# All fronts first, and two turns beside other stages, in a hybrid scan, convolution and attention kernel

## The chip, the cores and the metric

The kernel runs on one core of one Trainium2 chip. The metric is the device time of one execution in microseconds; the median of several runs is given.

## The reference

Four images of 96 channels and 64 x 64 pixels go through four layers. Only the first layer matters in detail here.

```python
# layer 0: x + conv_ref(group_norm(x))
u = silu(depthwise3x3(einsum('oc,bchw->bohw', Win, x)) + conv_b)      # 192 channels
xs = stack([u, u.T, flip(u), flip(u.T)])                              # 4 directions k
dts, Bs, Cs = split(einsum('bkdl,ked->bkel', xs, sel_w))              # 6 + 16 + 16
delta = softplus(dt_w @ dts + dt_b)
h[t] = h[t-1] * exp(delta * A) + (delta * u) * B[t]                   # 4096 steps, 192 x 16 states
y[k] = sum_n h * C
y = y0 + y1.T + flip(y2) + flip(y3).T + D * xs                        # directions summed
x = x + Wout @ layer_norm(y)
# layer 1: 1x1 convolution, depthwise 3x3, 1x1 convolution, residual
# layer 2: Fourier transform along the tokens, diagonal product, inverse, residual; quantised feed-forward
# layer 3: linear attention (k^T v first), residual; quantised feed-forward
```

## The kernel before

**The scan** is the backbone. For each image, direction and chunk of 512 positions there is a step (32 steps an image), and each step has 12 units of work. A unit makes two state tiles: POOL multiplies rep_g with rep_BC (L1266), ACT takes an exponential into PSUM (L1276), DVE runs the recurrence (L1285), DVE (L1290) or POOL (L1306) multiplies with C, and PE sums the states into ps_y (L1330). This makes 1536 units. Image 0's scan takes units 0 to 383, image 1's the next 384, and so on; directions go 0, 1, 3, 2, and 1, 3, 0, 2 for the last image. delta, du (delta times u), B and C are written to DRAM by the fronts and fetched from there, repeated over partitions, as rep_d, rep_g and rep_BC.

**The order is written out by hand.** `scans()` goes through the units; one pass of its loop is a slot. In each slot it emits the scan's own instructions, and then hands what is left to a planner. The planner holds a list of stages, and each stage a list of streams, generators that yield how much time of an engine the next piece takes (`pe(2.7, 1)`: 2.7 us of TensorE, one PSUM bank; `wait(10)`: not before ten slots later). Only the first stage of the list is worked on; up to `width` streams of it are active, the earlier ones first. A piece is emitted when the engine's allowance permits it. All engines and the SP queue keep the emitted order.

```python
RATE = 6.0                                                        # us of planned work a slot
SHARE = {"pe": (3.0, 3.2), "act": (2.4, 2.8), "dve": (1.5, 2.0)}  # gain a slot, most held
BANKS = {"mm": 3, "da": 4, "y": 1}                                # PSUM banks
```

**The stages of an image:** front (input convolution with the group norm, L550 and L559; then scan inputs, L588 to L627: sel and dt products, softplus on ACT and DVE, and stores of delta, du, bc), turn (the transposed directions 1 and 3 are put into row order, and directions 0 and the skip added), conv (scan outputs L697, output norm, layer 1's expansions L787 and rows L810), spectral twice and layer_2 (layer 2), product, layer_3.

**What holds a stage back.** `scanned[b]` counts the finished steps of image b. A turn waits until 24 steps are done (16 for the last image, whose second row group then waits piece by piece for up to 24). Chunk c of conv's scan outputs waits for 32 - c steps. Front(3) could not be placed before the end of image 0's scan, since delta, du and bc had three DRAM sets and image 3 used image 0's.

**A turn** has three row groups r of 64 channels. For each it loads the y rows of directions 1 and 3 into a buffer `ya` (two loads of 1 MB, L640), waits ten slots, and for each of eight chunks fetches rows of direction 0 and of the skip (L649, L650), makes two products into one bank (L655: the transposed read of `ya`; L657: the skips), copies the result on ACT (L661) and stores it.

**After the scan** the rest of image 3 (what is left of its conv, then layers 2 and 3) runs with all PSUM banks; this is called the tail.

Before the change the stage list is: rest of front(0), weights and group norm statistics, front(1), front(2), turn(0), conv(0), layers 2 and 3 of image 0, front(3), turn(1), conv(1), layer 2 of image 1, layer_3(1) with turn(2), conv(2), layer 2 of image 2, layer_3(2) with turn(3), conv(3); then the tail.

Of the kernel before, what the change touches and what calls it, by code (L numbers as in the profile page):

```python
# [27 lines left out]
B, C, H, W = 4, 96, 64, 64  # L28
L = H * W
K, NS, R, DI = 4, 16, 6, 192  # L30
# [3 lines left out]
CH = 512  # L34
NCH = L // CH
RPC = CH // W
# [15 lines left out]


WORK = {"weights": 47.0, "turn": 79.2, "front": 417.0, "conv": 447.0,
        "spectral": 111.2, "layer_2": 231.0, "product": 1.2, "layer_3": 153.6, "layer_3_turn": 232.8}
RATE = 6.0
SHARE = {"pe": (3.0, 3.2), "act": (2.4, 2.8), "dve": (1.5, 2.0)}
NQ, NG, NPAIR = 4, HID // 32, H // 2
# [37 lines left out]
def hybrid_kernel(ctx: ExitStack, tc: tile.TileContext, a: dict):  # L96
# [5 lines left out]
    mm = nc.tensor.matmul  # L102
    act = nc.scalar.activation
    load = nc.sync.dma_start
# [37 lines left out]
    def const(name, rows=slice(0, 128)):  # L142
        return cst[rows, CS[name]]
# [40 lines left out]
    def big(name):  # L184
        if last_room and turns(thirds) == "last":
            return last_room[0].tile([128, 6144], F32, name=name, tag="big", bufs=1)
        return bp.tile([128, 6144], F32, name=name, tag="big", bufs=2)
# [20 lines left out]
    def images(name, shape, zero=None, sets=2):  # L208

        out = []  # L210
        for i in range(sets):
            t = dram1.tile(shape, F32, name=f"{name}{i}")
            if zero is not None:
                zero(t)
            out.append(t)
        return out

    d_delta = [images(f"delta{k}_", [NCH, DI, CH], sets=3) for k in range(K)]
    d_du = [images(f"du{k}_", [NCH, DI, CH], sets=3) for k in range(K)]
    d_bc = [images(f"bc{k}_", [NCH, 2 * NS, CH], sets=3) for k in range(K)]  # L220

# [10 lines left out]
    def split(t):  # L234
        return t.rearrange("p (a b) -> p a b", a=RPC)
# [341 lines left out]

    def scan_inputs(b, u, o, c, done):

        i = b % 3  # L580
        if not done.issuperset([c] if o == 0 else range(NCH)):
            while not done.issuperset([c] if o == 0 else range(NCH)):
                yield wait(1)
            yield wait(2)
        ua, ub = u
        yield pe(1.8, 1)
        p = bank()
        mm(p, lhsT=sel[:, o, 0, :], rhs=view(ua, o, c), start=True, stop=False)  # L588
        mm(p, lhsT=sel[:, o, 1, :], rhs=view(ub, o, c), start=False, stop=True)

        yield ac(0.7)
        xd = tmp("xd")
        act(xd, p, AF.Identity, bias=col("one"))
        free()
        for e in (0, 1):
            later(d_bc[o + 2 * e][i][c], xd[64 * e : 64 * e + 2 * NS])
        for part in range(3):
            yield pe(0.9, 1, part > 0)
            p = bank()
            if part < 2:  # L600
                mm(p, lhsT=dtw[:, o + 2 * part, 0:128], rhs=xd, start=True, stop=True)  # L601
                at = [(slice(0, 128), o + 2 * part, slice(0, 128))]
            else:
                for e in (0, 1):
                    mm(p[64 * e : 64 * e + 64], lhsT=dtw[:, o + 2 * e, 128:DI], rhs=xd, start=True, stop=True)
                at = [(slice(64 * e, 64 * e + 64), o + 2 * e, slice(128, DI)) for e in (0, 1)]

            yield ac(0.65)
            z = tmp("z")
            act(z, p, AF.Abs)  # L610
            yield ac(0.65)
            act(z, z, AF.Exp, scale=-1.0)
            yield ac(0.65)
            act(z, z, AF.Ln, bias=1.0)  # L614
            yield dv(0.7)
            nc.vector.scalar_tensor_tensor(p, p, 0.0, z, ALU.max, ALU.add)  # L616
            yield dv(0.85)
            g = tmp("g")
            nc.vector.tensor_mul(split(g), split(p), view(ub if part == 2 else ua, o, c))
            for rows, k, ch in at:  # L620
                later(d_du[k][i][c][ch], g[rows])
            yield ac(0.6)
            nc.scalar.copy(z, p)  # L623
            free(behind=True)
            for rows, k, ch in at:
                later(d_delta[k][i][c][ch], z[rows])
        traced[b].add((o, c))  # L627

    def turn(b):


        im = b % 2
        early = b == B - 1
        while scanned[b] < (2 if early else 3) * NCH:
            yield wait(1)
        t = big("ya")
        for r in (2, 0, 1) if early else (0, 1, 2):
            lo = 64 * r
            for at, k in ((0, 1), (64, 3)):
                load(t[at : at + 64, :L].rearrange("p (c l) -> p c l", c=NCH),  # L640
                     d_y[k][im][:, lo : lo + 64, :].rearrange("c p l -> p c l"))

            rows = not (early and r == 2)
            held = slice(0 if rows else 64, 128)

            def fetch(c):
                u = t[:, L + c % 4 * CH : L + c % 4 * CH + CH]
                if rows:
                    load(u[:64], d_y[0][im][c, lo : lo + 64])  # L649
                load(u[64:], d_skip[b][c, lo : lo + 64])  # L650
                return u

            def added(p, of):
                c, u = of
                mm(split(p[:64]), lhsT=const("two")[:, :64],  # L655
                   rhs=t[:, :L].rearrange("p (w h) -> p h w", h=H)[:, c * RPC : (c + 1) * RPC, :], start=True, stop=False)
                mm(p[:64], lhsT=skips[held, r], rhs=u[held], start=False, stop=True)  # L657

            def stored(p, of):
                s = tmp("yrow")[:64]  # L660
                nc.scalar.copy(s, p[:64])  # L661
                later(d_yt[im][of[0]][lo : lo + 64], s)

            chunks = ahead(1, fetch, range(NCH))

            ready = (lambda n: scanned[b] >= 2 * NCH + min(n + 2, NCH)) if early and rows else (lambda n: True)
            yield wait(10)
            yield from in_turn(chunks, pe(2.7, 1), added, ac(0.6), stored, ready=ready)
            yield wait(2)
# [399 lines left out]
    def layers_2_and_3(b):  # L1069
# [83 lines left out]
        else:  # L1153
# [1 line left out]
        return spectra + [  # L1155
            Stage("layer_2", 4 if b == B - 1 else 3, *(layer_2(c) for c in range(NCH))),
            Stage("product", 1, product()),
            Stage("layer_3", 4 if b == B - 1 else 3, *(layer_3(c) for c in range(NCH))) if b not in (1, 2) else
            Stage("layer_3_turn", 4, turn(b + 1), *(layer_3(c) for c in range(NCH))),
        ]  # L1160

    def front(b):


        u, there, done = [], set(), set()

        def memory():
            u.extend([big("ua")[:, :L], big("ub")[:, :L]])
            if b > 0:
                yield from normalised(b, arriving(b), there)  # L1170
                return

            chunks = [(c, fetch_image(b, c, tmp)) for c in range(NCH)]
            load(cst[:, CS["grp"]], a["cst"][:, CS["grp"]])
            load(cols, a["cols"])
            first_weights()
            yield from group_norm(b, chunks)
            yield from normalised(b, chunks, there)

        streams = [memory()]  # L1180
        for c in range(0, NCH, 2):
            streams.append(input_conv(b, u, c, there, done))
            for e in (c, c + 1):
                streams.append(scan_inputs(b, u, 0, e, done))
        streams += [scan_inputs(b, u, 1, c, done) for c in range(NCH)]
        return [Stage("front", 3 if b == 0 else 4, *streams)]


# [5 lines left out]

    def middle(b):

        return ([] if b >= 2 else [Stage("turn", 1, turn(b))]) + conv_block(b)

    def plan():

        stats = (group_norm(b, arriving(b)) for b in range(1, B))
        out = [Stage("weights", 2, later_weights(), *stats)] + front(1) + front(2)
        out += middle(0) + layers_2_and_3(0) + front(3)
        for b in (1, 2):
            out += middle(b) + layers_2_and_3(b)
        return out

    def scans(stages):
# [13 lines left out]
        for number, step in enumerate(steps):  # L1222
            step["at"] = number % (K * NCH)
            u = 0
# [6 lines left out]

        def load_states(step, j):
            t = pair("rep_BC")
            of = d_bc[step["k"]][step["b"] % 3][step["c"], 8 * j : 8 * j + 8].rearrange("(s e) l -> s (e l)", e=2)
            load(t.rearrange("p e l -> p (e l)"), of.unsqueeze(0).to_broadcast([32, 4, 2 * CH]))
            step["BC"][j] = t

        def load_channels(step, i, name):
            t = pair(f"rep_{name}")
            of = (d_delta if name == "d" else d_du)[step["k"]][step["b"] % 3][step["c"], 64 * i : 64 * i + 64]  # L1240
            load(t.rearrange("p e l -> p (e l)"),
                 of.rearrange("(p e) l -> p (e l)", e=2).unsqueeze(1).to_broadcast([32, 4, 2 * CH]))
            step[name][i] = t
# [399 lines left out]
```

## Time and profile before

| | |
|---|---|
| median of 3 runs | 6344.4 us (6340.63 to 6344.61) |
| the profiled execution | 6358.61 us, span 6356.8 us |
| granted TensorE clock, mean | 0.834 |
| last recurrence of the scan ends | 5911 us into the span |
| HBM read, written | 861.88 MB, 237.44 MB |
| DMA queue of SP | 54.3% of 16 engines |
| L1266, one per unit | 1536 at 2365 ns |
| L1276, two per unit | 3072 at 690 ns |
| L1285, two per unit | 3072 at 1204 to 1272 ns |

The span runs from the first to the last instruction of the program. Busy times are of one profiled execution; its own time is compared with its own span, and it lies 14 us above the median. A window of the profile gives busy times between two moments of the span, counted in us from its start.

### The profile page before, as it was taken

How to read it: one execution, taken by the hardware profiler on the slowest of the kernel's cores; microseconds unless marked ns; L12 is line 12 of the kernel's file. 1: busy time of each engine (PE TensorE's matmuls, PEld its weight loads, DVE VectorE, ACT ScalarE, POOL GpSimd, SP SyncE). 2: the span in 40 equal slices, each digit the busy share in tenths (PEclk: the TensorE clock that was granted, in tenths of full speed). 3: DMA queues.
4: the chain of work that ended last, by engine and by line, in shares of the span. 5: the costliest groups of instructions: out<-in, count | busy, mean ns of one | idle time of the engine just before them, and what ended most of it. 6: DMA issues, size and time to landing. Idle time of an engine off the chain costs nothing. (4 is left out here: it accounts for less than half of the span.)

```text
span 6356.8 us, 84759 instructions
## 1 busy us (share of the span) xinstructions
PE 4685.7 (74%) x27692; PEld 1723.3 (27%) x27692; DVE 5490.6 (86%) x6059; ACT 4191.3 (66%) x8072; POOL 5169.6 (81%) x2743
## 2 busy tenths in 40 slices
PE   6732767756888776686469878767898777679998
PEld 2100212201222642121012236321222552112274
DVE  4979898998999989989989998888999999889245
ACT  5743777765666677877546656767666667666435
POOL 4857878779999899987899998898999988889100
PEclk9855978867998888797779987878899887789999
DMA  5654565667754554456776445456754554566201
GB/s 178 206 167 146 190 204 187 201 201 221 221 162 151 183 181 156 151 193 208 212 213 197 156 152 192 157 162 199 225 171 159 171 192 141 172 209 202 84 13 39
DMA packets 430397, 1100.47 MB, mean 173 GB/s; under 512 B 74138, under 2 KB 75904, under 8 KB 428804
## 3 DMA queue, kind: packets, MB, share of 16 engines
q1 hardware_dynamic: 429956, 1095.06, 54.3%
q8 instruction: 220, 3.60, 0.2%
q14 instruction: 221, 1.81, 0.1%
HBM read 861.88 MB, written 237.44 MB: 173 GB/s over the span
## 5 line engine op out<-in xcount | busy, mean ns | idle before, releaser
L1266 POOL TENSOR_TENSOR db<-rep_g,rep_BC 128x1024 f32<-128x1024 f32 x1536 | 3607.0, 2365 | 689.1 <-DVE hc L1285 323.5
L1276 ACT ACTIVATE ps_da<-rep_d,aneg 128x512 f32<-128x512 f32 x3072 | 2061.8, 690 | 478.8 <-DVE hc L1285 347.2
L1285 DVE TENSOR_TENSOR_SCAN ps_da<-ps_da,state,db 128x512 f32<-128x512 f32 x1568 | 1923.9, 1272 | 274.3 <-ACT state L1300 151.4
L1306 POOL TENSOR_TENSOR hc<-hc,rep_BC 128x1024 f32<-128x1024 f32 x640 | 1511.2, 2361 | 49.3 <-DVE hc L1285 4.5
L1285 DVE TENSOR_TENSOR_SCAN hc<-ps_da,state,db 128x512 f32<-128x512 f32 x1120 | 1371.7, 1266 | 71.3 <-issue 20.6
L1330 PE MATMUL ps_y<-hc,cst 128*32 128x512 f32 x6144 | 1014.4, 739 | 566.2 <-POOL hc L1306 261.1
L1290 DVE TENSOR_TENSOR hc<-ps_da,rep_BC 128x512 f32<-128x512 f32 x1792 | 1135.5, 675 | 0.0
L1300 ACT COPY state<-ps_da 128x1 f32<-128x1 f32 x1568 | 246.3, 157 | 456.9 <-DVE hc L1290 455.4
L1330 PEld LDWEIGHTS ps_y<-hc,cst 128*32 128x32 f32 x6144 | 145.8, 118 | 1210.5 <-issue 438.2
L810 PE MATMUL ps_mm<-h,wd 128*32 128x512 f32 x3120 | 357.0, 593 | 7.0 <-ACT r L155 7.0
L550 PE MATMUL ps_mm<-xp,taps 128*128 128x512 f32 x576 | 294.7, 656 | 54.9 <-ACT ua L552 15.1
L1285 DVE TENSOR_TENSOR_SCAN ps_da<-ps_da,db 128x512 f32<-128x512 f32 x224 | 261.3, 1212 | 39.5 <-ACT state L1300 24.7
L787 PE MATMUL ps_mm<-wd,w 128*32 128x512 f32 x1984 | 254.9, 630 | 29.3 <-DMA wd<-x 20.0
L601 PE MATMUL ps_mm<-xd,dtw 128*128 128x512 f32 x256 | 168.5, 751 | 73.6 <-ACT z L623 53.5
L791 ACT ACTIVATE h<-ps_mm 128x512 f32<-128x512 f32 x261 | 151.8, 597 | 66.5 <-PE ps_mm L787 64.5
L869 PE MATMUL ps_mm<-r,cst 128*128 128x512 f32 x222 | 152.3, 778 | 56.5 <-ACT acc L892 14.2
L616 DVE SCALAR_TENSOR_TENSOR ps_mm<-ps_mm,z 128x512 f32<-128x512 f32 x192 | 131.7, 686 | 70.8 <-ACT z L614 67.0
L1285 DVE TENSOR_TENSOR_SCAN hc<-ps_da,db 128x512 f32<-128x512 f32 x160 | 186.2, 1204 | 6.1 <-issue 3.1
L655 PE MATMUL ps_mm<-ya,cst 128*64 128x512 f32 x192 | 183.1, 1044 | 10.4 <-ACT acc L892 10.4
L610 ACT ACTIVATE z<-ps_mm 128x512 f32<-128x512 f32 x192 | 114.1, 595 | 111.7 <-PE ps_mm L601 59.2
L982 PE MATMUL ps_mm<-wa,xp 128*64 128x96 f32 x1728 | 134.9, 318 | 64.6 <-DVE d L987 61.9
L550 PEld LDWEIGHTS ps_mm<-xp,taps 128*128 128x128 f32 x576 | 115.9, 208 | 229.5 <-issue 159.9
(348 smaller groups left out, 6675.9 us busy)
## 6 DMA issues: line engine op xcount, KB each, us to landing
rep_BC<-bc SPq DMA_DIRECT2D x512, 512.0 KB
rep_g<-du SPq DMA_DIRECT2D x384, 512.0 KB
rep_d<-delta SPq DMA_DIRECT2D x384, 512.0 KB
y<-yt SPq DMA_DIRECT2D x512, 128.0 KB
du<-g SPq DMA_DIRECT2D x128, 256.0 KB
delta<-z SPq DMA_DIRECT2D x128, 256.0 KB
tab<-in_etab SPq DMA_DIRECT2D x112, 256.0 KB
ya<-y SPq DMA_DIRECT2D x24, 1024.0 KB
```

The costliest lines, as they stand in the source:

```text
L550: mm(p, lhsT=taps[:, t, 0:128], rhs=window(t, c + e), start=t == 0, stop=t == 8)
L601: mm(p, lhsT=dtw[:, o + 2 * part, 0:128], rhs=xd, start=True, stop=True)
L655: mm(split(p[:64]), lhsT=const("two")[:, :64], rhs=t[:, :L].rearrange("p (w h) -> p h w", h=H)[:, c * RPC : (c + 1) * RPC, :], start=True, ...
L787: mm(p[32 * n : 32 * n + 32], lhsT=w1[:, 32 * g : 32 * g + 32], rhs=xin[:, n : n + 15 : 2, 1 : W + 1], start=True, stop=True)
L810: mm(p[32 * n : 32 * n + 32], lhsT=held["wd"][:, groups[i], o, dx, :], rhs=here[i][:, :, dx : dx + W], start=dx == 0, stop=dx == 2)
L1266: nc.gpsimd.tensor_mul(x["db"], x["step"]["g"][x["i"]], both(x["step"]["BC"][x["j"]][:, 0]))
L1276: act(x["da"][e], x["step"]["d"][x["i"]][:, e], AF.Exp, scale=aneg[:, av : av + 1])
L1285: nc.vector.tensor_tensor_scan(x["h"][e][:, order], x["da"][e][:, order], x["db"][:, e, order], start, ALU.mult, ALU.add)
L1290: x["made"] = nc.vector.tensor_mul(x["hc"][:, e], x["h"][e], x["step"]["BC"][x["j"]][:, 1])
L1300: nc.scalar.copy(to[:, e : e + 1], x["h"][e][:, end : end + 1])
L1306: x["made"] = nc.gpsimd.tensor_mul(x["hc"], x["hc"], both(x["step"]["BC"][x["j"]][:, 1]))
L1330: done = mm(y[32 * q : 32 * q + 32], lhsT=const("stack"), rhs=x["hc"][:, e], start=first or (x["pass"] == 0 and x["j"] == 0), stop=last or ...
```

## The change

d_delta, d_du and d_bc get a set for every image. Front(3) comes right after front(2), before image 0's turn, and its stage is called front_turn: it holds turn(0) as a second stream, after the one that normalises the image, and five streams may be active instead of four. Turn(0) has no buffer of its own there. It uses the unused ends of front(3)'s two buffers `ua` and `ub` (columns 4096 to 6143 of each), so that the y rows lie in two halves of four chunks, each loaded by itself and each with a product of its own over half the columns; the direction 0 and skip rows go to a `tmp` buffer. In all turns the skips' product now comes first in its bank. Turn(1) becomes a stream of image 0's layer_3 stage, as turn(2) and turn(3) already were in those of images 1 and 2. No stage holds a turn alone any more.

```diff
-    d_delta = [images(f"delta{k}_", [NCH, DI, CH], sets=3) for k in range(K)]
-    d_du = [images(f"du{k}_", [NCH, DI, CH], sets=3) for k in range(K)]
-    d_bc = [images(f"bc{k}_", [NCH, 2 * NS, CH], sets=3) for k in range(K)]
+    d_delta = [images(f"delta{k}_", [NCH, DI, CH], sets=B) for k in range(K)]
+    d_du = [images(f"du{k}_", [NCH, DI, CH], sets=B) for k in range(K)]
+    d_bc = [images(f"bc{k}_", [NCH, 2 * NS, CH], sets=B) for k in range(K)]
...
-    def turn(b):
+    def turn(b, rooms=()):
...
-        t = big("ya")
+        if rooms:
+            of_rows = [t[:, L:] for t in rooms]
+        else:
+            t = big("ya")
+            of_rows = [t[:, :L]]
+        each = L // len(of_rows)
         for r in (2, 0, 1) if early else (0, 1, 2):
             lo = 64 * r
-            for at, k in ((0, 1), (64, 3)):
-                load(t[at : at + 64, :L].rearrange("p (c l) -> p c l", c=NCH),
-                     d_y[k][im][:, lo : lo + 64, :].rearrange("c p l -> p c l"))
+            for n, part_of in enumerate(of_rows):
+                cs = slice(n * each // CH, (n + 1) * each // CH)
+                for at, k in ((0, 1), (64, 3)):
+                    load(part_of[at : at + 64].rearrange("p (c l) -> p c l", l=CH),
+                         d_y[k][im][cs, lo : lo + 64, :].rearrange("c p l -> p c l"))
...
-                u = t[:, L + c % 4 * CH : L + c % 4 * CH + CH]
+                u = tmp("yu") if rooms else t[:, L + c % 4 * CH : L + c % 4 * CH + CH]
...
-                mm(split(p[:64]), lhsT=const("two")[:, :64],
-                   rhs=t[:, :L].rearrange("p (w h) -> p h w", h=H)[:, c * RPC : (c + 1) * RPC, :], start=True, stop=False)
-                mm(p[:64], lhsT=skips[held, r], rhs=u[held], start=False, stop=True)
+                wide_of = W // len(of_rows)
+                mm(p[:64], lhsT=skips[held, r], rhs=u[held], start=True, stop=False)
+                for n, part_of in enumerate(of_rows):
+                    mm(split(p[:64])[:, :, n * wide_of : (n + 1) * wide_of], lhsT=const("two")[:, :64],
+                       rhs=part_of.rearrange("p (w h) -> p h w", h=H)[:, c * RPC : (c + 1) * RPC, :], start=False,
+                       stop=n == len(of_rows) - 1)
...
-            Stage("layer_3", 4 if b == B - 1 else 3, *(layer_3(c) for c in range(NCH))) if b not in (1, 2) else
+            Stage("layer_3", 4 if b == B - 1 else 3, *(layer_3(c) for c in range(NCH))) if b == B - 1 else
             Stage("layer_3_turn", 4, turn(b + 1), *(layer_3(c) for c in range(NCH))),
...
+        if b == B - 1:
+            return [Stage("front_turn", 5, streams[0], turn(0, rooms), *streams[1:])]
         return [Stage("front", 3 if b == 0 else 4, *streams)]
...
-        return ([] if b >= 2 else [Stage("turn", 1, turn(b))]) + conv_block(b)
+        return conv_block(b)
...
-        out = [Stage("weights", 2, later_weights(), *stats)] + front(1) + front(2)
-        out += middle(0) + layers_2_and_3(0) + front(3)
+        out = [Stage("weights", 2, later_weights(), *stats)] + front(1) + front(2) + front(3)
+        out += middle(0) + layers_2_and_3(0)
```

## What is predicted

> **What bounds the kernel now.** I read the page's engine shares first, then the slices, then the busy time by stage. One pass of the scan loop is called a slot here: 1536 of them, each with one L1266 multiplication on POOL two slots ahead. Counting those gives the slot of any instruction.
>
> ```profile
> PE 4685.7 (74%) x27692; PEld 1723.3 (27%) x27692; DVE 5490.6 (86%) x6059; ACT 4191.3 (66%) x8072; POOL 5169.6 (81%) x2743
> ...
> DVE  4979898998999989989989998888999999889245
> ...
> POOL 4857878779999899987899998898999988889100
> ```
>
> DVE is the busiest engine and stays at 8 or 9 tenths until the scan ends, in the 38th slice. Behind it lies a tail where POOL has nothing to do. The busy time of each engine by stage (columns: window, its length, then busy us and instructions of PE, PEld, DVE, ACT, POOL, clock, DMA share, GB/s; the windows run from the first to the last instruction of a stage):
>
> ```profile
> 1001.00:1384.00 383.00, 274.57 (x848) 77.79 (x848) 349.92 (x386) 290.36 (x548) 308.39 (x163) 0.81 0.61 196
> 1384.00:1593.00 209.00, 110.59 (x328) 18.98 (x328) 184.21 (x191) 105.19 (x224) 192.45 (x107) 0.69 0.71 212
> ...
> 2554.00:2710.00 156.00, 102.76 (x310) 25.66 (x308) 147.79 (x154) 131.16 (x254) 146.59 (x78) 0.74 0.47 151
> 2710.00:3086.00 376.00, 268.72 (x840) 77.08 (x840) 346.12 (x382) 288.89 (x549) 304.75 (x164) 0.81 0.62 199
> 3086.00:3300.00 214.00, 111.80 (x336) 19.32 (x336) 182.85 (x190) 102.66 (x212) 194.23 (x103) 0.69 0.72 209
> 4271.00:4505.00 234.00, 175.76 (x464) 40.34 (x464) 197.18 (x206) 166.65 (x332) 199.71 (x108) 0.81 0.67 198
> 5469.00:5710.00 241.00, 176.15 (x476) 38.47 (x476) 198.67 (x208) 168.58 (x332) 202.96 (x106) 0.82 0.64 192
> 5710.00:5911.00 201.00, 177.95 (x846) 52.61 (x838) 189.86 (x205) 129.35 (x259) 191.57 (x102) 0.94 0.60 190
> 5911.00:6100.00 189.00, 182.99 (x1333) 62.64 (x1332) 21.53 (x37) 66.43 (x103) 0.00 (x0) 1.00 0.18 59
> ```
>
> In order: front(2), turn(0), layer_3(0), front(3), turn(1), layer_3(1) with turn(2), layer_3(2) with turn(3), the part of conv(3) that lies beside the scan, and the rest of conv(3) after it. Window minus DVE busy is the time that DVE lost: 30 us in front(3), 25 in turn(0), 31 in turn(1), 8 in layer_3(0), 37 and 42 in the two stages where a turn and a layer share the beside work. The last row is the other bound: PE is busy for 183 of 189 us at full clock, so what conv(3) leaves over when the scan ends is paid in PE time.
>
> What a slot costs with nothing beside it is seen between a turn's first loads and its first matmul (same columns):
>
> ```profile
> 3086.00:3116.60 30.60, 9.76 (x41) 1.19 (x42) 30.60 (x33) 14.22 (x24) 29.52 (x13) 0.50 0.87 258
> ...
> 3213.60:3259.50 45.90, 9.76 (x44) 1.01 (x40) 34.71 (x36) 17.78 (x39) 36.52 (x21) 0.54 0.69 177
> ```
>
> Ten slots in 30.6 us, 3.06 each, with DVE busy throughout: an empty slot wastes no DVE time. So **shifting work between slots earns nothing**; only DVE's lost time and the tail can change. The second row is the same kind of stretch at the third row group of turn(1): 11 us lost. The waits within turn(0)'s window (who, for whom: us, times, longest) say how a turn loses time:
>
> ```profile
> ACT yrow L661 <- PE ps_mm L657: 42.9, 20, 14.0
> ACT state L1300 <- DVE hc L1290: 42.5, 20, 5.0
> ...
> PE ps_mm L657 <- DMA ya<-skip: 19.1, 4, 10.1
> ...
> POOL db L1266 <- DMA rep_BC<-bc: 14.5, 3, 9.1
> DVE ps_da L1285 <- ACT state L1300: 14.1, 6, 8.9
> ...
> DVE ps_da L1285 <- POOL db L1266: 9.3, 7, 2.7
> ```
>
> Two routes: the 2 MB of y rows delay the scan's rep_BC, POOL waits 14.5 us and DVE 9.3 behind it; and PE waits for skip rows, ACT waits for PE, and DVE loses 14.1 waiting for ACT.
>
> **What the Trainium skill says.** "DMA: Bandwidth & Descriptors", section on queues, rings and completion order, says that an engine consumes a ring's descriptors in order, so a small load issued behind 2 MB is late. The trace agrees: in layer_3(1)'s stage PE waits 12.5 us for an xc load issued behind turn(2)'s y rows. "TensorE: Matmul & The Clock Gate", section on the array's architecture, says that ACT and DVE queues are strict FIFO and that matmuls keep their order; the ACT and DVE waits above are of that kind. The same page, on the clock gate, says that an idle PE falls to half clock: 0.50 in the empty slots above, 0.94 beside conv(3).
>
> **The change, part by part.**
>
> *Buffers.* A fourth set for delta, du and bc removes the reason for front(3) to come after image 0's scan. The same stores go out; cost nothing, at any place.
>
> *front(3) moves* from slots 669–759 to right behind front(2), which ends at slot 294. All its 91 slots of matmuls, activations, DVE work and stores on SP go along. Fronts 1, 2 and 3 take 384, 383 and 376 us in three different places, so the move itself costs 0 (−7 to +7).
>
> *turn(0) beside it.* Its gate, 24 steps of image 0, falls at slot 288 plus 5 for sums and store, so it starts with the stage at about 296. In the planner's units a front's first 50 slots hold 133 us of TensorE work of an allowed 150 (3.0 a slot); the turn adds 24 x 2.7 = 65. (133 + 65) / 3 is 66, so the joint stage takes some 91 + 16, about 110 slots, where front and turn took 91 + 60. DVE's lost time in it is the open term. Added up, it is 30 + 25 = 55. In layer_3 with a turn the measured 37 and 42 stand against 8 + (25 to 31) = 33 to 39, so that pair was about additive. In a front, though, POOL is busy only 305 of 376 us, and 9.3 us of the turn's loss came through a late POOL. I take half of that as covered: **50, −5 us**. Bounds: 30, all of the turn hidden (−25), and 80, the turn's PE waits also stalling the activations that the front feeds to DVE (+25).
>
> *Smaller edits.* turn(0)'s y rows lie in halves, so its 48 L655 instructions of 512 columns become 96 of 256: the same columns, so 1.04 us splits in two, and 48 more issues, hidden since PE is busy for 0.7 of a front; uncovered, at no more than the 0.6 us that a whole 512-column L657 instruction takes, 48 x 0.6 = 29 us of PE time. Twelve 512 KB loads replace six of 1 MB: six more SP issues at 0.6 us, covered by a ten-slot wait. The skip rows go to a tmp buffer, so SP can stand behind whoever last used it, with the scan's rep loads queued behind SP; no row shows this, and it lies within the bound of 80. That the skips product now comes first only moves PE's wait.
>
> *turn(1) beside layer_3(0).* The joint front stage ends near slot 406, 50 later than turn(0) did; layer_3(0) then starts near 677, and turn(1)'s gate is 384 + 293 = 677. They coincide: loss 37 to 42, where 8 + 31 were lost. 0 (−5 to +8).
>
> *Then the lead is given back.* conv(1) starts near slot 737 instead of 819, 82 earlier. layer_3(1) runs from about 1008 to 1050, but turn(2)'s gate is 768 + 293 = 1061: ten empty slots at no DVE loss, then the turn alone. 8 + 25 to 31 instead of 37, so −1 (−4 to +2). conv(2) starts near 1123 instead of 1147. turn(3) starts near 1394 and runs into its own gate: the last two pieces of its second row group need 24 steps of image 3, slot 1152 + 293 = 1445. After them come two and ten slots of waiting, eight pieces, two slots. It ends near 1471 instead of 1475, so **of 82 slots about five reach conv(3)**.
>
> *The tail.* conv(3) has 59 slots beside the scan and gets 64. Its loss there is 11 us now. Its output pieces are gated by the scan, but its expansions follow five slots earlier. conv beside the scan does some 2 us of PE work of its own a slot (178 us less 57 slots at 0.75 for L1330, over 59 slots, is 2.3), so five slots carry 9 to 11 us out of the PE-bound row: **−9** (−13 to −3).
>
> Sum: −5 + 0 + 0 − 1 − 9, about **−14 us**. The profiled execution took 6358.6 (span 6356.8, 1.8 around it), which gives about 6345 for one like it; it lies 14 above the median of the runs, 6344.4, so I forecast **6331**.
>
> **Rivals.**
>
> *Deep overlap.* The front's loss lies in its first half, where DVE is busy 3.5 of 4.0 us a slot; if the turn's waits fall into those same gaps, 33 us are lost, not 55: −22 − 9, 6313. For it: POOL's slack, and a warmer PE clock than the turn's 0.69. Against it: the joint layer stages show no such thing.
>
> *The turn starves the front; slower.* Place: slots 296 to 406. A late skip row holds PE, at whose 3.0 a slot the front already stands at 2.7; ACT waits in order, and so do the scan's exponentials. The price is the joint layer stage's DVE share, 197 of 234, 84%, applied here: 110 slots hold 110 x 3.06 + 0.8 x 91 = 409 us of DVE work, 409 / 0.84 = 487, 78 lost instead of 55: +23 − 9, 6358. It decides from 77 lost on, when it outweighs the tail by 13 us. Against it: a front's streams load almost nothing, so the 12.5 us wait for xc has no counterpart after the first images.
>
> *The lead is lost entirely.* If the joint stage or turn(3)'s pieces slip by five slots, conv(3) starts where it did: additive losses, no tail gain, 6344.
>
> **Chances.** 0.2% is 13 us, about what a measurement of this kernel tells from no change. Forecast 0.50 (6318 to 6344, a little over half of it beyond 13 us faster), deep overlap 0.15, lead lost 0.12, starved 0.23. Faster 0.42, same 0.34, slower 0.24. The range 6306 to 6362 holds the forecast with most of both outer cases.
>
> **What would show it.** In the profile after: L655 matmuls of image 0 within the L550 ones of image 3, done by slot 360; the joint stage 440 to 465 us long, with DVE losing about 50; turn(1) at slot 687, with layer_3(0); ten slots near 1055 with no beside work; conv(3)'s first L697 near slot 1475 instead of 1480; the tail after the last scan 436 us instead of 446. The forecast is wrong if the stage loses over 77 or under 35, or if the tail moves by over 15.

## The result, and the profile after

The changed kernel is **slower: 6382 us against 6341 as medians of five runs each, ratio 1.0074 (1.0059 to 1.0088)**. That is 42 us between the medians and 47 by the ratio; 6331 was forecast. The changed kernel's profiled execution has a span of 6373.4 us. The profile of before that the prediction read (6356.8) was a long one for its kernel; a second one, of the unchanged kernel (e0), has 6334.8, close to its median, and it stands for before in what follows. In the changed kernel's file the lines are shifted: L1279 is the POOL product that was L1266, L1289 the exponential, L1298 the recurrence, L1313 the state copies, L663 and L665 the turn's two products (skips, y rows), L707 the scan outputs.

The engine shares and slices of the page after, three lines to be held against those of before:

```profile
PE 4674.7 (73%) x27740; PEld 1718.3 (27%) x27740; DVE 5482.4 (86%) x6059; ACT 4193.3 (66%) x8072; POOL 5169.4 (81%) x2743
...
DVE  5979899987899999888999989998999889888245
...
POOL 4757878877779999888999989998999898889200
```

The engines did the same work, 48 more PE instructions apart (the halves of the y rows). In the 9th and 10th slices, where the joint stage begins, DVE is at 8 and 7 tenths instead of 9 and 8. The windows by stage, first before (e0; columns: window, length, busy us and instructions of PE, PEld, DVE, ACT, POOL, clock, DMA share, GB/s): turn(0), layer_3(0), front(3), turn(1), layer_3(1) with turn(2), layer_3(2) with turn(3), conv(3) beside the scan, what is left of conv(3) up to its last matmul.

```profile
1380.00:1589.00 209.00, 110.35 (x328) 18.82 (x328) 184.41 (x191) 105.63 (x226) 192.89 (x107) 0.70 0.72 212
2549.00:2704.00 155.00, 98.67 (x310) 24.91 (x309) 148.14 (x154) 131.00 (x254) 146.74 (x79) 0.81 0.47 154
2704.00:3082.00 378.00, 272.43 (x840) 77.99 (x840) 346.26 (x382) 288.72 (x550) 304.74 (x164) 0.79 0.61 198
3082.00:3294.00 212.00, 109.86 (x336) 19.04 (x336) 183.11 (x191) 103.35 (x213) 195.24 (x103) 0.71 0.71 211
4254.00:4484.00 230.00, 169.98 (x463) 38.33 (x456) 194.67 (x204) 165.77 (x331) 197.78 (x106) 0.84 0.68 200
5444.00:5683.00 239.00, 177.17 (x472) 38.72 (x472) 198.63 (x208) 168.52 (x332) 203.11 (x107) 0.81 0.65 193
5683.00:5887.00 204.00, 180.85 (x850) 53.03 (x842) 190.29 (x204) 129.59 (x259) 192.01 (x102) 0.92 0.59 188
5887.00:6059.00 172.00, 168.84 (x1160) 51.12 (x1158) 11.28 (x21) 62.75 (x97) 0.00 (x0) 1.00 0.19 63
```

After: front(3) with turn(0), layer_3(0) with turn(1), layer_3(1), the empty slots before turn(2)'s gate, turn(2), layer_3(2) with turn(3), conv(3) beside the scan, what is left of it.

```profile
1380.00:1881.00 501.00, 357.24 (x1088) 99.88 (x1082) 421.89 (x460) 338.76 (x651) 384.47 (x204) 0.81 0.67 207
2839.00:3072.00 233.00, 174.00 (x464) 39.50 (x464) 192.87 (x205) 166.87 (x338) 200.55 (x111) 0.82 0.67 199
4019.00:4175.00 156.00, 106.23 (x312) 26.61 (x312) 148.59 (x155) 132.55 (x258) 148.91 (x80) 0.74 0.46 152
4175.00:4202.00 27.00, 9.38 (x41) 1.22 (x40) 27.00 (x30) 14.30 (x27) 26.92 (x14) 0.56 0.43 141
4202.00:4421.00 219.00, 109.68 (x332) 19.09 (x328) 184.18 (x191) 104.04 (x223) 200.17 (x110) 0.69 0.69 201
5389.00:5697.00 308.00, 192.30 (x534) 40.42 (x534) 257.86 (x264) 195.47 (x390) 258.26 (x138) 0.74 0.56 171
5697.00:5935.00 238.00, 195.18 (x956) 56.63 (x957) 216.22 (x232) 144.50 (x290) 222.20 (x118) 0.89 0.56 183
5935.00:6098.00 163.00, 161.31 (x1085) 51.63 (x1083) 10.78 (x20) 61.16 (x95) 0.00 (x0) 1.00 0.21 66
```

Length minus DVE busy is what DVE lost. The joint stage lost 79 us where turn(0) and front(3) lost 25 + 32. The empty slots lost nothing: 27.00 of 27.00. The last rows show the gain: what is left of conv(3) after the scan takes 163 us instead of 172, with 161 us of PE work instead of 169, and the whole tail fell from 447.7 to 438.8. The first 45 us of the joint stage show where its loss begins (who waits, for whom: us in total, times, longest):

```profile
POOL db L1279 <- DMA rep_BC<-bc: 15.1, 1, 15.1
DVE ps_da L1298 <- ACT state L1313: 14.6, 2, 13.7
ACT xp L530 <- DMA x<-in_x: 14.2, 4, 9.9
```

ACT stands for image 3's pixels. Three of the eight pixel loads were issued ahead of the turn's y rows and five behind them; the first of those behind is the wait of 9.9 us. The scan's state copies and exponentials stand behind it on ACT, and DVE behind those for 14.6 us. POOL at the same time waits 15.1 for rep_BC.

The loss of DVE by group of stages, in us, from one profile each (made as above, stage by stage; e1 to e8 are the experiments below). e5's profile is the longest of its nine runs, 25 us above their median.

| | e0 (before) | after | e1 | e3 | e5 | e6 | e8 |
|---|---|---|---|---|---|---|---|
| front(3), turn(0) | 56 | 79 | 58 | 66 | 44 | 79 | 43 |
| layer_3(0), turn(1), layer_3(1), turn(2) | 71 | 82 | 72 | 80 | 75 | 79 | 75 |
| layer_2, three images | 58 | 66 | 73 | 65 | 67 | 63 | 58 |
| layer_3(2), turn(3), conv(3) beside the scan | 54 | 72 | 78 | 65 | 67 | 61 | 46 |
| conv and spectral, images 0 to 2 | 129 | 124 | 132 | 130 | 151 | 128 | 146 |
| everything up to the scan's end | 564 | 618 | 603 | 597 | 599 | 603 | 569 |
| tail, its length | 447.7 | 438.8 | 436.9 | 435.5 | 438.9 | 447.8 | 447.1 |

Between e0 and after the first four groups add 60 us and the conv and spectral stages give 5 back, so DVE lost 54 us more in all. It was also busy 7 us less before the scan's end, so the scan ended 47 later, and the tail gave 9 back: 39 in these two profiles.

### The profile page after: what moved, and what is told of

Same layout as the page of the kernel before. It is cut to its first block, busy times and chain, and to the rows that moved or that the text cites. A ratio compares the mean times of both kernels' runs of the same rounds, so it can differ in the third digit from the quotient of the medians.

```text
span 6373.4 us, 84876 instructions
## 1 busy us (share of the span) xinstructions
PE 4674.7 (73%) x27740; PEld 1718.3 (27%) x27740; DVE 5482.4 (86%) x6059; ACT 4193.3 (66%) x8072; POOL 5169.4 (81%) x2743
## 5 line engine op out<-in xcount | busy, mean ns | idle before, releaser
L1279 POOL TENSOR_TENSOR db<-rep_g,rep_BC 128x1024 f32<-128x1024 f32 x1536 | 3607.8, 2365 | 716.5 <-DVE hc L1298 329.3
L1289 ACT ACTIVATE ps_da<-rep_d,aneg 128x512 f32<-128x512 f32 x3072 | 2062.3, 690 | 445.3 <-DVE hc L1298 329.0
L1298 DVE TENSOR_TENSOR_SCAN ps_da<-ps_da,state,db 128x512 f32<-128x512 f32 x1568 | 1923.9, 1272 | 244.5 <-ACT state L1313 136.5
L1298 DVE TENSOR_TENSOR_SCAN hc<-ps_da,state,db 128x512 f32<-128x512 f32 x1120 | 1371.6, 1266 | 107.3 <-issue 49.2
L1343 PE MATMUL ps_y<-hc,cst 128*32 128x512 f32 x6144 | 1009.3, 736 | 580.3 <-POOL hc L1319 258.9
L1313 ACT COPY state<-ps_da 128x1 f32<-128x1 f32 x1568 | 246.4, 157 | 450.0 <-DVE hc L1303 446.0
L1343 PEld LDWEIGHTS ps_y<-hc,cst 128*32 128x32 f32 x6144 | 145.6, 118 | 1240.4 <-issue 445.6
L1298 DVE TENSOR_TENSOR_SCAN ps_da<-ps_da,db 128x512 f32<-128x512 f32 x224 | 261.0, 1210 | 49.1 <-ACT state L1313 40.3
L616 DVE SCALAR_TENSOR_TENSOR ps_mm<-ps_mm,z 128x512 f32<-128x512 f32 x192 | 131.5, 685 | 83.1 <-ACT z L614 69.2
L1298 DVE TENSOR_TENSOR_SCAN hc<-ps_da,db 128x512 f32<-128x512 f32 x160 | 186.0, 1203 | 5.8 <-ACT ps_da L1289 3.0
L707 PE MATMUL ps_mm<-ypart,cst 128*128 128x512 f32 (+1 forms) x272 | 156.3, 698 | 23.9 <-DMA ypart<-yt 23.9
```

The source lines that it names most:

```text
L707: mm(p, lhsT=const(name, slice(0, s.shape[0])), rhs=s, start=n == 0, stop=n == len(of) - 1)
L1279: nc.gpsimd.tensor_mul(x["db"], x["step"]["g"][x["i"]], both(x["step"]["BC"][x["j"]][:, 0]))
L1289: act(x["da"][e], x["step"]["d"][x["i"]][:, e], AF.Exp, scale=aneg[:, av : av + 1])
L1298: nc.vector.tensor_tensor_scan(x["h"][e][:, order], x["da"][e][:, order], x["db"][:, e, order], start, ALU.mult, ALU.add)
L1313: nc.scalar.copy(to[:, e : e + 1], x["h"][e][:, end : end + 1])
L1343: done = mm(y[32 * q : 32 * q + 32], lhsT=const("stack"), rhs=x["hc"][:, e], start=first or (x["pass"] == 0 and x["j"] == 0), stop=last or ...
```

## Experiments

Each run was measured beside the kernel before, whose median was then 6332 to 6335 us and not 6341. Differences to the changed kernel are therefore taken from the ratios; going by their intervals, two ratios that differ by less than about 0.002, 13 us, aren't told apart.

**e0, the kernel before once more.**

> The kernel before, unchanged, for a second profile. Both theories: ratio 1.000 within its interval. The first profile of before took 6358.6 us, 18 above the median of its runs; if that profile was a slow sample, this one's span is near 6340 and shows in which stages the 18 us lay. Then the joint stage's 34 us over the sum of its parts (499 against 465) is not the whole change of 42, and some 10 to 20 us are elsewhere.

Measured: 6336.6 against 6333.6, ratio 1.0004 (0.9995 to 1.0013); span 6334.8. The long profile had lost 22 us more of DVE time, half of it in the spectral stage of image 1 (33 instead of 22) and the rest in small parts everywhere. So the joint stage's excess is 23 us, and it isn't the whole.

**e1, turn(0) by itself behind front(3).**

```diff
-            return [Stage("front_turn", 5, streams[0], turn(0, rooms), *streams[1:])]
+            return [Stage("front", 4, *streams), Stage("turn", 1, turn(0))]
```

> After, with turn(0) as a stage of its own behind front(3), in its own buffer. By the planner conv(2) starts at slot 1121 as in after, so the end is the same and only the joint stage is undone. Theory 'starved front': DVE loses 30 + 25 us here instead of 80, so about 25 us less than after: 6357, ratio to before 1.0025. Rival 'place': front(3) early costs by itself, or the lead does, through the order of what follows; then 6375 to 6385 as after.

Measured: 6369.3, ratio 1.0058 (1.0043 to 1.0074), 10 us less than after, which is not clear of noise, and between the two expectations. The stages did what was expected:

```profile
1378.00:1758.00 380.00, 272.09 (x848) 77.16 (x840) 349.38 (x385) 290.97 (x548) 303.49 (x161) 0.81 0.61 201
1758.00:1969.00 211.00, 113.40 (x336) 19.21 (x336) 184.04 (x191) 103.28 (x223) 197.57 (x109) 0.67 0.72 212
```

Front(3) in its early place loses 31 us and the turn 27, as before: the move itself costs nothing. But most of the slowdown stayed: undoing the joint stage took 21 us of DVE's loss out of it, while layer_2, the conv and spectral stages and layer_3(2) with turn(3) and conv(3) lost more than in after, and all that is lost fell by 15 only. So neither theory is enough alone: the joint stage has a share of the 54 us, and what follows it has the rest.

**e2, turn(1) by itself behind layer_3(0).**

```diff
-            Stage("layer_3", ...) if b == B - 1 else
+            Stage("layer_3", ...) if b in (0, B - 1) else
...
-        return conv_block(b)
+        return ([Stage("turn", 1, turn(1))] if b == 1 else []) + conv_block(b)
```

> After, with turn(1) as a stage of its own behind layer_3(0). By the planner conv(2) starts at slot 1121 as in after; layer_3(1) then overlaps turn(2) again. Theory 'starved front': nothing but the exchange of one pair for another, 6382 (6375 to 6388). Rival 'turn(1) in layer_3(0) costs': 8 to 20 us less than after, 6362 to 6374.

Measured: 6395.1, ratio 1.0101 (1.0088 to 1.0114), 17 us more than after and outside both expectations. Apart, layer_3(0) and turn(1) lost 44 us in the profile, together in after 40: turn(1) beside layer_3(0) is thus no cost of the change. Layer_2 of image 1, which now began at another slot, lost 29 us instead of 15: that pointed at the slots in which stages begin.

**e3, the rows fetched early.**

```diff
+            if ready(0):
+                chunks = chain([next(chunks)], chunks)
             yield wait(10)
             yield from in_turn(chunks, pe(2.7, 1), added, ac(0.6), stored, ready=ready)
```

> After, with the first two chunks' rows of direction 0 and skip fetched right behind the y rows, ten slots before they are used, in all turns. Theory 'PE waits for the skip rows, ACT behind PE, DVE behind ACT': the 34 us of PE waits for yu in the joint stage go, and DVE's loss there falls from 80 to about 55; with 3 to 8 us from each of the three other turns, 6335 to 6360. Rival 'DMA congestion or PE's own work': the same bytes and matmuls, 6375 to 6385.

Measured: 6360.9, ratio 1.0048 (1.0034 to 1.0061), 16 us less than after. PE's waits for skip rows (yu) fell, those of ACT for L665 went from 45.0 to 29.5, and the joint stage's loss from 79 to 66. In the joint stage of after, and then of e3:

```profile
PE ps_mm L663 <- DMA yu<-skip: 27.7, 6, 9.3
DVE ps_mm L616 <- ACT z L614: 11.9, 4, 3.2
DVE ps_mm L616 <- ACT state L1313: 11.1, 3, 9.1
...
PE ps_mm L663 <- DMA yu<-skip: 11.1, 6, 3.8
DVE ps_mm L616 <- ACT z L614: 8.3, 3, 3.0
DVE ps_mm L616 <- ACT state L1315: 2.1, 2, 1.2
```

The chain from skip rows over PE and ACT to DVE is real, and it ends in the front's own work: L616, DVE's part of its softplus, waited 10.4 us for ACT instead of 23.0, which is nearly all of the 13.

**e4, layer_2 begun in one phase of the scan's step.**

```diff
+        if b in (0, 1, 2):
+            spectra.append(Stage("product", 1, hold(lambda: clock[0] % 12 == 2)))
```

`hold` is a stream that waits one slot at a time until its condition holds.

> After, with each layer_2 of images 0 to 2 held until the slot number divided by 12 leaves 2, the phase in which it starts after spectral in the before kernel's images 0 and 2 (a step of the scan has 12 slots, and its rep loads go out in fixed ones). conv(2) and the end keep their slots. Theory 'phase': in the profiles so far DVE loses 14 to 17 us in a layer_2 of that phase and 22 to 28 in one of another; images 0 and 2 fall from 24 and 26 us to about 15 each, 15 to 20 less than after: 6365, ratio to before 1.0045. Rival 'chance': the loss is not tied to the phase, 6376 to 6388.

Measured: 6388.2, ratio 1.0084 (1.0070 to 1.0098): no gain in time, so as the rival said. In its one profile (6364.4, the shortest of its runs) the three layer_2 lost, in their first 68 slots:

```profile
2595.00:2841.00 246.00, 169.99 (x652) 54.80 (x652) 226.56 (x248) 187.91 (x373) 225.89 (x119) 0.79 0.45 151
3815.00:4059.00 244.00, 170.25 (x652) 55.38 (x652) 229.00 (x248) 187.87 (x375) 227.61 (x121) 0.79 0.46 152
5142.00:5384.00 242.00, 166.07 (x652) 53.49 (x652) 226.00 (x249) 189.19 (x374) 225.81 (x120) 0.82 0.47 154
```

That is 19, 15 and 16 us, where after lost 26, 15 and 26. But the slots in which they were held lost 8 us themselves, and the spectral stage of image 1, which came later for it, 28 instead of 23. The loss inside layer_2 fell; that the kernel gains by it isn't shown.

**e5, e3 with turn(0) started once image 3 is normalised.**

```diff
+        def once_normalised():
+            while len(there) < NCH:
+                yield wait(1)
+            yield from turn(0, rooms)
...
-            return [Stage("front_turn", 5, streams[0], turn(0, rooms), *streams[1:])]
+            return [Stage("front_turn", 5, streams[0], once_normalised(), *streams[1:])]
```

> e3 (rows fetched early), and turn(0) starts only when front(3)'s image is normalised, so that its first 2 MB of y rows stand behind the image's loads. Theory 'loads in ring order': the 10 us that ACT waits for the image and part of the 15 us that POOL waits for rep_BC in the first ten slots go; the joint stage loses 55 instead of 66 us, 6350. Rival 'the same bytes delay something else': as e3, 6361.

Measured: 6350.9, ratio 1.0036 (1.0022 to 1.0050), as expected in time, but not clearly less than e3. The joint stage lost even less than the 55 us expected. Its row, and its waits in the first 45 us:

```profile
1379.00:1856.00 477.00, 351.00 (x1096) 98.66 (x1096) 432.55 (x472) 344.79 (x661) 396.76 (x212) 0.83 0.71 219
...
POOL db L1286 <- DMA rep_BC<-bc: 10.3, 2, 5.5
ACT xp L530 <- DMA x<-in_x: 5.0, 2, 3.0
DVE ps_da L1305 <- ACT state L1320: 2.5, 2, 2.1
```

44 us in 477 are less than front(3) and turn(0) one after the other (56) lost. So a turn does hide in part in a front, once its loads stand behind the front's and its rows are there in time. (L1286 is here the POOL product, L1305 the recurrence, L1320 the state copies.) The theory accounts for some 8 of the 21 us that the stage lost less than in e3: those in its first 45 us, 6.8 lost instead of 14.7. The other 13 came later in the stage, and no run says why. Nor did the kernel keep them in this profile: its conv and spectral stages, which for images 0 and 1 began two to four slots later, lost 21 us more than e3's, and in all the two profiles lost about the same, 599 and 597.

**e6, the rest of the lead given up.**

```diff
-        return conv_block(b)
+        return ([Stage("product", 1, hold(lambda: clock[0] >= 1147))] if b == 2 else []) + conv_block(b)
```

> After, with conv(2) held until slot 1147, where it started in before: the lead that is left is given up, and from there on the order is that of before (conv(3) at slot 1477 instead of 1469). Theory 'the lead costs in layer_2 and turn(3) more than it earns in the tail': DVE loses 27 us less (layer_2 of image 2 26 to 17, layer_3(2) with turn(3) and conv(3) 72 to 54), the tail is 9 longer, the 26 empty slots cost nothing: 6364, ratio 1.0045. Rival 'lead earns': 9 us more than after, 6391.

Measured: 6365.4, ratio 1.0053 (1.0041 to 1.0065), 13 us less than after (17 between the medians), with a tail that is 9 longer and 4 us lost in the empty slots. Starting conv(2) 26 slots earlier therefore costs this kernel more than it earns, by an amount just clear of noise.

**e7, the early rows in the kernel before.** The edit of e3.

> The kernel before, with the first two chunks' rows of direction 0 and skip fetched right behind the y rows in every turn, as in e3. Theory 'PE waits for skip rows, ACT behind PE, DVE behind ACT': 3 to 6 us from each of four turns, 6316 to 6325, ratio 0.997 to 0.998. Rival 'only the joint stage had such a loss': 6336, ratio 1.000.

Measured: **6320.1, ratio 0.9980 (0.9971 to 0.9989): faster than both kernels.** The time is as the theory said, its place is not: instead of 3 to 6 us in each turn, most of it is in layer_3(2) with turn(3), 28 us lost instead of 40; turn(0) and turn(1) lose 2 and 3 less, layer_3(1) with turn(2) none. This changes the reading of e3. The same two lines win 13 us here and 16 in the changed order, so in time little of what they win belongs to the change, although in the joint stage they win 13 us of DVE's loss and in turn(0) alone 2.

**e8, e5 and e6 together.**

> e5 (rows early, turn(0) once front(3)'s image is normalised) and e6 (conv(2) held until slot 1147) together. Theory 'two independent costs, the loads at the joint stage's start and the lead that moves layer_2 and turn(3) to worse slots': 6382 - 31 - 17 = 6334, ratio to before 1.000 (0.998 to 1.002). Rival 'the two are one, or chance': no better than the better of them, 6350.

Measured: 6343.1, ratio 1.0008 (0.9999 to 1.0016), within the range that the first theory gave and below either of the two: the gains of e5 and e6 add up, to 42 us. But the early rows among them help the unchanged order as well. Beside e7, the unchanged order with the same rows early, e8 is still 18 us slower. By the two profiles it lost 12 us more than e7 in the conv and spectral stages of images 0 to 2, 7 in the slots in which conv(2) is held and 6 in the stages of layer_3(0) to turn(2), and 11 less in front(3) with turn(0); why the conv and spectral stages lose more is open.

**e9 and e10, the turn's y rows behind layer_3's first loads,** in e7 and in e8.

```diff
+    def behind(stream):
+        yield wait(1)
+        yield from stream
...
-            Stage("layer_3_turn", 4, turn(b + 1), *(layer_3(c) for c in range(NCH))),
+            Stage("layer_3_turn", 4, behind(turn(b + 1)), *(layer_3(c) for c in range(NCH))),
```

> e7 (before with rows early), and in layer_3_turn the turn's y rows go out one slot after the first three layer_3 chunks' loads instead of ahead of them. Theory 'loads in ring order': the 9 to 12 us that PE waits for xc at the start of these two stages go, 4 to 8 us of DVE's loss in each, 6308 to 6314, ratio 0.996 to 0.997. Rival 'the wait only moves to rep_BC': as e7, 6320, 0.998.

> e8 with the turns behind the first layer_3 loads, as in e9, in three stages (the second of them has the turn gated for long, so nothing changes there). Theory: 4 to 8 us in each of two stages, 6318 to 6328, ratio 0.998 to 0.999. Rival: as e8.

Measured: e9 6328.5, ratio 0.9992 (0.9981 to 1.0003); e10 6333.1, ratio 0.9994 (0.9983 to 1.0004). e10 is 9 us below e8, where 8 to 16 were expected, with intervals that overlap, so a gain over e8 isn't shown. e9 missed: it isn't better than e7. Its two windows, layer_3(1) with turn(2) and then layer_2 of image 2:

```profile
4244.00:4468.00 224.00, 170.09 (x461) 38.64 (x453) 197.41 (x205) 165.42 (x329) 197.91 (x106) 0.83 0.69 204
...
5191.00:5446.00 255.00, 176.14 (x692) 59.32 (x692) 228.39 (x250) 192.65 (x392) 228.82 (x127) 0.78 0.45 151
```

The stage itself lost 27 us instead of e7's 36, as the theory says. But conv(2) and all behind it began one slot later, and layer_2 of image 2 lost 27 instead of 17, conv(2) and spectral of image 2 some 18 more. So the best order that holds the change, e10, isn't better than the unchanged one with its rows early, e7.

## Why the prediction was wrong

**Right:** the order of the work. The joint stage ran from slot 296 to 410 (said: 406), conv(1) began at 739 (737), turn(2) stood at its gate at 1061, conv(2) began at 1121 (1123), conv(3) at 1469 with its first L707 at 1472 (1475). Of 80 slots of lead eight reached the end. Moving front(3) cost nothing (e1: 380 us). The empty slots before turn(2) cost no DVE time, though the 26 in which conv(2) is held lost 4 in e6 and 7 in e8. Turn(1) with layer_3(0) lost 40 us instead of 36, inside its bounds, and e2 shows that it wasn't what cost. The tmp buffers for the skip rows did not hold SP: it stood 0.7 us for them in the turn.

**Right by luck: the tail.** It gave 8.9 us, where 9 was said. But eight slots came, not five, and each carried about 1 us of conv(3)'s PE work instead of 2: beside the scan PE was busy 195 us in after and 181 in e0, and six of these 14 us are L1343's own at the 0.75 a slot that the prediction used. Two errors cancelled. The prediction's row 5911 to 6100 also reached 17 us into the next layer, so less of conv(3) was left to win than it showed, and its terms sum to −15, not −14.

**Wrong, first term: the loss in the joint stage, 50 said, 79 measured.** It was the rival with the starved front, which named 78 lost from the 84% of the joint layer stages; the stage ran at 422 of 501, 84%. The step that gave −5 held: POOL's slack covered the turn. What failed is the other route, over ACT, which the sum took along from the two stages apart. DVE's waits in the joint stage of after, and then in e1's front(3) and turn(0) apart:

```profile
DVE ps_da L1298 <- ACT state L1313: 36.2, 13, 13.7
...
DVE ps_da L1298 <- ACT state L1313: 19.0, 14, 3.7
...
DVE ps_da L1298 <- POOL db L1279: 7.2, 6, 2.2
```

In all DVE waited 62 us for ACT instead of 32, and for POOL not at all instead of 13. Two things in the prediction led there. First, that the turn's PE waits spread to the activations that the front feeds to DVE was left to the bound of 80. They did spread: e3 took 13 us out of the stage, nearly all of them waits of L616 in the front. Second, my reason against the rival was that a front's streams load almost nothing. But five of image 3's eight pixel loads go out just behind the turn's 2 MB of y rows. The first 45 us, in after and then for front(3) alone in e1:

```profile
1380.00:1425.00 45.00, 30.93 (x88) 10.28 (x84) 30.36 (x33) 22.38 (x45) 29.55 (x16) 0.73 0.70 194
1378.00:1423.00 45.00, 36.50 (x124) 12.60 (x117) 38.44 (x40) 28.89 (x55) 39.77 (x22) 0.85 0.56 188
```

14.6 us lost instead of 6.6 are 8 more. With rows early and the turn's loads behind the pixels, in e5, the stage lost 44 and the forecast's direction for this term, a gain, came true, in the stage and not in the whole kernel.

**Wrong, second: the loss of a stage was taken along unchanged when the stage moved.** The sum held −1 for layer_3(1) and turn(2) apart; they lost 7 more (turn(2) alone 35, above the 25 to 31 I had from two cases). It held nothing for layer_2 (8 more), for layer_3(2) with turn(3) (10 more) and for conv(3) beside the scan (8 more). Two causes can be read in part. At slot 1494 of conv(3) PE waits for a chunk of the scan's outputs whose first load went out only 9 us before; ACT waits 7.3 us behind it, and DVE loses 8 there. Likely conv(3) had caught up with the chunk's gate; no run tests it. And layer_2 loses by the slot in which it starts. Its first 68 slots before (e0, images 0, 1 and 2, starting at slots 555, 1019, 1347, which leave 3, 11 and 3 when divided by 12; these starts are counted in the profile and lie one above the kernel's own count, so the remainder 2 of e4's edit is a 3 here):

```profile
2296.00:2540.00 244.00, 165.57 (x677) 53.21 (x675) 229.15 (x250) 191.19 (x378) 227.81 (x122) 0.83 0.46 154
3998.00:4251.00 253.00, 171.16 (x691) 57.70 (x690) 228.06 (x250) 191.76 (x377) 224.08 (x117) 0.81 0.46 148
5189.00:5437.00 248.00, 172.27 (x681) 54.73 (x679) 229.41 (x248) 192.11 (x391) 228.39 (x127) 0.80 0.46 151
```

and after (slots 611, 939, 1322, leaving 11, 3 and 2):

```profile
2584.00:2836.00 252.00, 172.21 (x692) 58.14 (x690) 226.28 (x250) 191.55 (x377) 223.57 (x117) 0.81 0.44 148
3774.00:4015.00 241.00, 166.37 (x678) 54.98 (x676) 226.37 (x249) 191.06 (x377) 227.04 (x121) 0.82 0.46 156
5129.00:5386.00 257.00, 173.21 (x668) 54.21 (x660) 231.01 (x252) 191.55 (x376) 231.38 (x123) 0.78 0.47 151
```

With 3 left over 15, 19 and 15 us are lost, with 11 left over 25 and 26, with 2 left over 26. In the ten profiles from before and after to e7, the fourteen layer_2 that start with 3 left over lose 15 to 19 us, the nine with 11 left over 24 to 29 (a tenth, in e9, lost 22). The likely reason is where its loads and matmuls fall among the scan's rep loads, which go out in fixed slots of the twelve; that was only argued. e6, which puts image 2's layer_2 back at slot 1347, found 16 lost instead of 26 there and 13 us less in all. e4, which started all three with 3 left over (4, 12 and 1 slots later than in after), had the smaller losses in layer_2 and no gain in time. What decides for the other stages stays open.

**The lead wasn't worth its price.** The prediction asked only how much of it reaches conv(3). e6 shows that giving up the last 26 slots wins 13 us although the tail loses 9.

## What to carry to other kernels

When two streams are put beside each other, look at what each loads in its first slots and in which order the one queue takes it: here the joint stage lost 44 us with the turn's loads behind the front's and 66 with them ahead, though the stages after it took the gain back. Fetch what a matmul needs when its neighbours are fetched, not when it is due; a late 128 KB row held PE, ACT behind it and DVE behind that, and two added lines made the unchanged order 0.2% faster (e7). A stage's loss isn't a property of the stage: against a periodic backbone it depends on the slot it starts in, so read it at several starts before carrying it over, and judge a mended stage by the whole kernel's time. Measure a remedy in the old order too: what helps both isn't a cost of the change. Count a lead only if something at the end is short of it.

## What the runs showed of the hardware that I had not expected

ACT's wait for a 192 KB load issued behind 2 MB came to 9.9 us at a DMA share of 0.67 in the stage, and one load for the scan, rep_BC, was waited for 15.1 us in the same place. A shift of a whole stage by one slot (3.8 us), with the same instructions in it, moved DVE's loss in layer_2 of image 2 from 17 to 27 us (e7 against e9, one profile each).
